# Where the softmax sums stand in a round, and where their division is made: a two-layer graph network on one core

## The chip, the cores and the metric

One core of a Trainium2 chip runs the whole program. The metric is the device time of one execution in microseconds (us). The core has a matrix engine (TensorE, "PE" in the profile), a vector engine (VectorE, "DVE"), a scalar engine (ScalarE, "ACT"), a general engine (GpSimd, "POOL") and a sync engine (SyncE, "SP") that issues DMAs. Each works through its own queue of instructions in order, and they wait for each other by semaphores. TensorE writes its results to PSUM; VectorE and ScalarE read them there[...].

## The reference, cut to what matters

64 independent batches of 256 tokens with 512 features each go through two layers; all arithmetic is float32. H is 8 heads of 64 features.

```
# layer 0: attention with a mask that all batches share
q, k, v = x @ Wq + bq, x @ Wk + bk, x @ Wv + bv          # in 8 heads of 64
scores  = q k^T / 8 + (1 - adj) * -1e9                   # 256 x 256 for each head
attn    = softmax(scores over the keys)
x       = layernorm(x + (attn v) @ Wo + bo)
# layer 1: additive attention, one head
h  = x @ W ;  s1 = h . a[:512] ;  s2 = h . a[512:]
e  = leaky_relu(s1[:, None] + s2[None, :], 0.2) * adj
x  = layernorm(x + elu(softmax(e) h + beta * h))
```

## The kernel before, in words

The program is written as a list of operations per batch. `Plan.op` (L76) records each with its engine, an estimated duration, what it reads and writes, and, for TensorE, a *turn*. `Plan.place` (L107) then puts all operations of all 64 batches into one order, and `emit` writes that order out; on the chip every engine's queue follows it. Three rules of `place` matter:

- TensorE follows the turns strictly (L160) until 70 of its operations are left; those last ones are free. A turn is (round, place in `ROUND`), set by `turn` (L477): `later` says in which round an operation of batch n is done, counted from n, and `ROUND` (L23) in which order within a round.
- Every other operation gets a due time, counted back from the TensorE operations that need it (L123); what no TensorE operation needs is due 15 us after what it reads (L131). Each engine takes what can start first, and among those that can start equally soon the one due first.
- Buffers are taken from slots (L236): 8 PSUM banks (tag "ps"), 9 large tiles in SBUF for xT, qT, kT, V, oT and others, 5 for x, and so on. An operation that finds no slot free waits. A change of TensorE's array shape (the `mode` of an operation) counts 0.25 us.

A round before the change works on four batches at once. In the order of `ROUND`, for round r, with the batch in brackets: mix (r-1), scores (r), o (r-1), spread (r-2), x (r+1), sums (r), v (r), logits (r-1), u (r-2), q (r+1), k (r+1), attention (r-1).

What these are:

- **x**: two blocks of 128 tokens are transposed (`tr_x`, L498), copied out by ScalarE (L501), and GpSimd makes three sums of quarters and a difference in place from them (`token_sums`, L350; L360 in the profile). Later GpSimd adds the bias of the output to x (L503).
- **q, k, v, o, u**: products with the weights, and **spread**: the product of layer 1's attention with x. All six go through `project` (L369): seven products of quarters of the matrices in place of eight (Strassen's scheme in Winograd's form), into three PSUM banks, `ps_chain`, `ps_cross` and `ps_pair`. ScalarE copies and VectorE adds collect the quarters (L519, L522, L528; for o, VectorE adds to x, L702).
- **scores** (two operations, for four heads each): k times q with a contraction of 64, so two matmuls stand side by side in the rows of the array (mode "rows", L576). VectorE adds the mask (L583), ScalarE takes the exponential (L585), and GpSimd adds the two halves of the keys (`both`, L587). Keys lie on the partitions, so a softmax sum is a sum over partitions.
- **sums** (`denominators`, L591): products with a matrix of ones, four side by side (mode "sums", L599), give the softmax sums of the eight heads in one bank, `ps_den`. VectorE takes the reciprocal (L603); ScalarE adds up `ps_den` and the reciprocal for a check of their range (L606); a DMA stores the reciprocals in DRAM (L609), and two more load them back, spread over the partitions, as `inv_all` (`everywhere`, L613).
- **mix** (two operations): attention weights times v, 64 columns a head, two side by side (mode "columns", L553), into `ps_pv`. VectorE multiplies `ps_pv` by `inv_all` on its way out to `oT` (L619); that is the division of the softmax. GpSimd then makes o's sums of quarters from `oT`.
- **logits**: after o, each block of 128 tokens is normalised (`norm`, L455: L458 and L459 on VectorE, L462 and L463 on GpSimd, L466 on VectorE, L468 on ScalarE). VectorE takes four products with sums (L717, into `junk`, with `s` the result). TensorE transposes `s` (`tr_s`, L727), and a chain over L733, L735, L737, L739, L741, L744, L746 makes layer 1's attention.
- **attention**: its transposition (`tr_a`, L755), copied out by ScalarE (L759), with four sums on GpSimd (L770).
- At the end of a batch, after u: L803 to L806, a second `norm`, and the store (L809).

If a check of the sums' range fails, another path (`attention_by_queries`) computes everything again. With these inputs it isn't run.

Of the kernel before, what the change touches and what calls it, by code (L numbers as in the profile page):

```python
# [19 lines left out]
ALPHA = 0.2  # L20
NEG = -1000000000.0

ROUND = ("mix", "scores", "o", "spread", "x", "sums", "v", "logits", "u", "q", "k", "attention")  # L23
SAFE = 1e15


# [196 lines left out]
def gnn_two_layers(ctx: ExitStack, tc: tile.TileContext, x, adj, Wq, bq, Wk, bk, Wv, bv, Wo, bo, W, a, beta, out):  # L223
    nc = tc.nc
# [23 lines left out]
    plan = Plan(slots)  # L248
    stay = []
    A = slice(None)  # L250

    def sb(tag, shape, name):
        return Buf(sb_pool, tag, [P] + shape, name)

    def ps(shape, name):
        return Buf(ps_pool, "ps", [P] + shape, name)
# [11 lines left out]
    def blk(t):  # L268
        return slice(t * P, (t + 1) * P)

    def half(i):
        return slice(i * F, (i + 1) * F)
# [141 lines left out]
    def residual_bias():  # L414
        bo_sb = for_now(bo, 0, "bo")
        acc = ps([D], "ps_b")

        def pe():
            for c in range(C):
                nc.tensor.matmul(acc[A], bv_sb[:, c:c + 1].to_broadcast([P, P]), wo_sb[:, c, :], start=c == 0,  # L420
                                 stop=c == C - 1)

        plan.op("PE", 3440, pe, [wo_sb], [acc], claims=[res_sb])
        plan.op("DVE", 690, lambda: nc.vector.tensor_add(res_sb[A], acc[A], bo_sb[A]), [acc, bo_sb], [res_sb])  # L424
        return weight_sums(wo_sb, "so_sb", "POOL", [res_sb])
# [46 lines left out]
    def batch(b, at, general=False):  # L472

        X = sb("x", [NT, D], f"x_{b}")
        n = b or 0

        def turn(what):  # L477

            later = {"x": -1, "q": -1, "k": -1, "scores": 0, "v": 0, "sums": 0, "mix": 1, "o": 1, "logits": 1,
                     "attention": 1, "spread": 2, "u": 2}[what]  # L480
            plan.turn = (n + later, ROUND.index(what if b != 0 or what != "sums" else "logits"))

        plan.op("SP", 2800, lambda: nc.sync.dma_start(X[A], x[at].rearrange("o (t p) d -> p (o t) d", p=P)), [],
                [(X, (t, i)) for t in range(NT) for i in range(2)], first=b == 0)
# [6 lines left out]
        V = sb("full", [NT, D], f"v_{b}")  # L491
# [14 lines left out]
        if b == 0:  # L506
            plan.turn = (0, ROUND.index("spread"))
            left["o"] = residual_bias()
        turn("x")
        for t in range(NT):  # L510
            tr_x(t)
# [24 lines left out]
        def val():  # L536
            turn("v")
            project(lv, right, False, [V], *gather(lambda q: (lambda: V[:, q[1], half(q[0])], (V, q))))


        oT = sb("full", [C, N], f"oT_{b}")

        def mixed(pT, g, onto, reads=()):

            turn("mix")
            acc = ps([2, N], "ps_pv")

            def pe():
                for i in range(2):
                    for k in range(NT):  # L550
                        for s in range(2):
                            h = 4 * g + 2 * i + s
                            nc.tensor.matmul(acc[s * HD:(s + 1) * HD, i, :], V[:, k, h * HD:(h + 1) * HD],  # L553
                                             pT[h][:, k, :], start=k == 0, stop=k == NT - 1)

            plan.op("PE", 1740, pe, [(V, (g, 0)), (V, (g, 1))] + pT[4 * g:4 * g + 4] + list(reads), [acc],
                    mode="columns", claims=[oT])
            plan.op("DVE", 690, lambda: onto(acc), [acc] + list(reads), [(oT, g)])

        def attention_by_keys():  # L560

            pT = [sb("half", [NT, N], "pT") for h in range(H)]
            both = [sb("half", [2, N], "both") for c in range(C)]
            inv, everywhere = sb("half", [N], "inv"), sb("full", [C, N], "inv_all")
            rows = Buf(dram_pool, "rows", [H, N], "rows")

            def scores(g):
                turn("scores")
                acc = [ps([NT, N], "ps_sc") for _ in range(4)]

                def pe():
                    for i in range(0, 4, 2):
                        for k in range(NT):
                            for s in range(2):
                                h, r = 4 * g + i + s, s * HD
                                nc.tensor.matmul(acc[i + s][:, k, :], kT[r:r + HD, h // 2, blk(k)],  # L576
                                                 qT[r:r + HD, h // 2, :], start=True, stop=True)

                plan.op("PE", 1740, pe, [(m, (g, j)) for m in (qT, kT) for j in range(NT)], acc, mode="rows",
                        claims=pT[4 * g:4 * g + 4] + both[2 * g:2 * g + 2])  # L580
                for i in range(4):
                    h = 4 * g + i
                    plan.op("DVE", 690, lambda h=h, i=i: nc.vector.tensor_add(pT[h][A], acc[i][A], maskT_sb[A]),  # L583
                            [acc[i], maskT_sb], [pT[h]])
                    plan.op("ACT", 620, lambda h=h: nc.scalar.activation(  # L585
                        pT[h][A], pT[h][A], AF.Exp, scale=1.0 / HD ** 0.5), [pT[h]], [pT[h]])
                    plan.op("POOL", 725, lambda h=h: nc.gpsimd.tensor_tensor(  # L587
                        both[h // 2][:, h % 2, :], pT[h][:, 0, :], pT[h][:, 1, :], ALU.add),
                        [pT[h]], [(both[h // 2], h % 2)])

            def denominators():  # L591
                turn("sums")

                acc = ps([N], "ps_den")

                def pe():
                    for s in range(2):
                        for c in range(C):
                            nc.tensor.matmul(acc[32 * c:32 * c + 32, :], ones[:, 16 - 16 * s:48 - 16 * s],  # L599
                                             both[c][:, s, :], start=s == 0, stop=s == 1)  # L600

                plan.op("PE", 1000, pe, both, [acc], mode="sums", claims=[inv])
                plan.op("DVE", 1750, lambda: nc.vector.reciprocal(inv[A], acc[A]), [acc], [inv])  # L603
                for i, m in enumerate((acc, inv)):
                    junk = sb("half", [N], "junk")
                    plan.op("ACT", 600, lambda i=i, m=m, junk=junk: nc.scalar.activation(  # L606
                        junk[A], m[A], AF.Identity, accum_out=range_sb[:, i, b:b + 1]), [m],
                        [junk, (range_sb, (i, b))])
                plan.op("SP", 60, lambda: nc.sync.dma_start(rows[A], inv[0:P:P // H, :]), [inv], [rows])  # L609
                for s in range(2):  # L610
                    def spread(s=s):
                        r = rows[A]
                        nc.sync.dma_start(everywhere[s * HD:(s + 1) * HD], bass.AP(  # L613
                            tensor=r.tensor, offset=r.offset + s * N, ap=[[0, HD], [2 * N, C], [1, N]]))

                    plan.op("SP", 1500, spread, [rows], [(everywhere, s)])

            def mix(g):
                mixed(pT, g, lambda acc: nc.vector.tensor_mul(  # L619
                    oT[:, 2 * g:2 * g + 2, :], acc[A], everywhere[:, 2 * g:2 * g + 2, :]), [everywhere])  # L620

            scores(0)
            scores(1)
            val()
            denominators()
            mix(0)
            mix(1)

        def attention_by_queries():
# [32 lines left out]
            pT = [sb("half", [NT, N], "pT") for h in range(H)]  # L662
# [20 lines left out]
            for g in range(2):  # L683
                for h in range(4 * g, 4 * g + 4):
                    flip(h)
                mixed(pT, g, lambda acc, g=g: nc.vector.tensor_copy(oT[:, 2 * g:2 * g + 2, :], acc[A]))

        turn("q")
        qk(lq, bq_sb, qT)
# [2 lines left out]
        if general:  # L692
            attention_by_queries()
        else:
            attention_by_keys()
# [4 lines left out]
        def onto(q, acc):  # L700
            i, j = q
            plan.op("DVE", 420, lambda: nc.vector.tensor_add(  # L702
                X[:, j, half(i)], X[:, j, half(i)], acc[1]()), [acc[0], (X, (j, i))], [(X, (j, i))])
# [10 lines left out]
        for t in range(NT):  # L714
            for i in range(2):
# [4 lines left out]
                    mode="two")  # L720
# [45 lines left out]
        sums = [(lambda i=i: S[:, i]) for i in range(4)]  # L766
# [27 lines left out]
        u = sb("full", [NT, D], f"u_{b}")  # L794
# [43 lines left out]
    with tc.If(again != 0):  # L838
# [3 lines left out]
        with tc.For_i(0, B, 1) as i:  # L842
            for tile_ in stay:
                tile_.parts = {}
            plan = Plan({**slots, "half": slots["half"] - 1})
# [33 lines left out]
```

## Time and profile before

| | us |
|---|---|
| median of three executions | 2874.97 (2874.73 to 2876.3) |
| the profiled execution: its span | 2874.1 |
| one steady round | 44.07 |

Busy time in the profiled execution:

| engine | busy us | share | instructions |
|---|---|---|---|
| TensorE, matmul | 2838.8 | 99% | 20373 |
| TensorE, weight load | 2489.0 | 87% | 20373 |
| VectorE | 2072.5 | 72% | 4514 |
| ScalarE | 1385.9 | 48% | 3393 |
| GpSimd | 1757.7 | 61% | 2522 |

Lines of the profile name an engine, a line of the kernel, an operation, what it writes and reads, and the shapes as partitions x elements; "x8" means eight instructions. In a timeline the first column is the start and the second the duration; neighbours of one kind are merged into one line. Matmuls overlap in the pipeline, so the time that one group costs is read from its start to the next group's start. DMA moves 39 GB/s on the mean, and the granted TensorE clock is 0.996 of full speed.

### The profile page before, as it was taken

Reading aid. Unit: us, or ns where it says so; the run is one execution under the profiler, and the core shown is the slowest. Engines: PE = TensorE matmul, PEld = TensorE weight load, DVE = VectorE, ACT = ScalarE, POOL = GpSimd, SP = SyncE. Lnnn points to the kernel's source line nnn. Section 1 sums busy time; section 2 is a strip of 40 time slices with the busy share of each in tenths; the row PEclk is TensorE's granted clock in tenths of the full one; section 3 lists DMA queues with packets and bytes.
Section 4 is the critical chain, followed back from the end, with each engine's and each line's share of the span. In section 5 each row is a group of like instructions: output and inputs, shape, how many; then the busy total and the mean of one; then the engine's idle time right before and its main releaser. Section 6 shows DMA issues by size and latency. Waiting matters only on the chain.

```text
span 2874.1 us, 54166 instructions
## 1 busy us (share of the span) xinstructions
PE 2838.8 (99%) x20373; PEld 2489.0 (87%) x20373; DVE 2072.5 (72%) x4514; ACT 1385.9 (48%) x3393; POOL 1757.7 (61%) x2522
## 2 busy tenths in 40 slices
PE   8999999999999999999999999999999999999996
PEld 7888888888888888888888888888888888888885
DVE  5777776776777777767777777677776776776766
ACT  3454544444444445444545454444454445544443
POOL 6665565665655656656656556566565565665654
PEclk9999999999999999999999999999999999999998
DMA  3101111111011110110110111101101111011100
GB/s 133 31 30 38 38 38 38 31 41 42 31 38 41 35 38 33 43 38 30 38 45 31 38 38 38 38 31 38 45 31 38 40 35 38 31 45 38 31 23 30
DMA packets 75417, 111.02 MB, mean 39 GB/s; under 512 B 5904, under 2 KB 39440, under 8 KB 75152
## 3 DMA queue, kind: packets, MB, share of 16 engines
q1 hardware_dynamic: 75024, 107.50, 11.3%
q8 instruction: 163, 2.67, 0.4%
q14 instruction: 102, 0.84, 0.1%
q0 software_dynamic: 128, 0.01, 0.0%
HBM read 73.41 MB, written 34.08 MB: 37 GB/s over the span
## 4 chain that ended last, share of the span: by engine, by line
PE 98%; DVE 1%; POOL 0%; issue 0%; DMA 0%; ACT 0%; POOLq 0%; DVEq 0%
PE ps_chain L387 18%; PE ps_chain L382 15%; PE ps_pair L387 11%; PE ps_cross L387 11%; PE ps_cross L382 10%; PE ps_pair L382 10%; PE ps_sc L576 8%; PE ps_pv L553 8%; PE ps_den L599 2%; PE tr_x L498 2%; PE tr_a L755 1%; PE tr_s L727 1%; DVE junk L717 0%; DMA beta_sb<-in_L_gnn_beta_dram 0%; PE ps_b L420 0%
## 5 line engine op out<-in xcount | busy, mean ns | idle before, releaser
L585 ACT ACTIVATE pT<-pT 128x512 f32<-128x512 f32 x512 | 312.1, 630 | 448.0 <-DVE pT L583 444.3
L587 POOL TENSOR_TENSOR both<-pT 128x256 f32<-128x256 f32 x512 | 357.9, 731 | 24.3 <-ACT pT L585 24.0
L462 POOL TENSOR_SCALAR rs<-mv 128x1 f32<-128x1 f32 x256 | 55.9, 219 | 504.3 <-DVE mv L459 504.3
L583 DVE TENSOR_TENSOR pT<-ps_sc,maskT_sb 128x512 f32<-128x512 f32 x512 | 322.5, 681 | 22.4 <-PE ps_sc L576 22.3
L717 DVE SCALAR_TENSOR_TENSOR junk<-x,wa_sb 128x512 f32<-128x512 f32 x256 | 282.3, 1154 | 0.4 <-ACT x L468 0.3
L770 POOL TENSOR_TENSOR att_sums<-attT 128x128 f32<-128x128 f32 x128 | 58.8, 459 | 323.6 <-ACT attT L759 318.6
L576 PE MATMUL ps_sc<-qT,kT 64*128 64x256 f32 x2048 | 238.4, 382 | 0.0
L468 ACT ACTIVATE x<-x,nmr,rs 128x512 f32<-128x512 f32 x256 | 200.7, 808 | 72.1 <-DVE nmr L466 63.6
L553 PE MATMUL ps_pv<-pT,v 128*64 128x256 f32 x2048 | 235.1, 382 | 0.0
L576 PEld LDWEIGHTS ps_sc<-qT,kT 64*128 64x128 f32 x2048 | 192.8, 187 | 44.1 <-issue 24.2
L553 PEld LDWEIGHTS ps_pv<-pT,v 128*64 128x64 f32 x2048 | 141.3, 137 | 75.4 <-issue 10.4
L619 DVE TENSOR_TENSOR oT<-ps_pv,inv_all 128x512 f32<-128x512 f32 x128 | 88.5, 691 | 163.6 <-PE ps_pv L553 163.6
L458 DVE BATCH_NORM_STATS2 bn<-x 128x6 f32<-128x512 f32 x256 | 164.0, 680 | 2.3
L503 POOL TENSOR_TENSOR x<-x,res_sb 128x512 f32<-128x512 f32 x128 | 160.5, 1276 | 7.3 <-DVE res_sb L424 7.3
L360 POOL TENSOR_TENSOR oS<-oT 128x256 f32<-128x256 f32 x128 | 94.0, 734 | 108.3 <-DVE oT L619 103.3
L463 POOL TENSOR_TENSOR rs<-rs,neg_half 128x1 f32<-128x1 f32 x256 | 144.7, 565 | 21.4
L360 POOL TENSOR_TENSOR xS<-xT 128x256 f32<-128x256 f32 x128 | 140.8, 1100 | 8.1 <-ACT xT L501 3.1
L382 PE MATMUL ps_chain<-xS,sq_sb 128*128 128x128 f32 x1024 | 135.8, 276 | 0.0
L382 PE MATMUL ps_chain<-xS,sk_sb 128*128 128x128 f32 x1024 | 135.2, 275 | 0.0
L702 DVE TENSOR_TENSOR x<-x,ps_chain 128x256 f32<-128x256 f32 x256 | 101.4, 416 | 44.9 <-PE ps_chain L387 38.2
L387 PE MATMUL ps_chain<-so_sb,oS 128*128 128x256 f32 x512 | 131.5, 379 | 0.0
L387 PE MATMUL ps_chain<-sw_sb,yS 128*128 128x256 f32 x512 | 131.5, 379 | 0.0
(192 smaller groups left out, 7546.0 us busy)
## 6 DMA issues: line engine op xcount, KB each, us to landing
x<-in_x_dram SPq DMA_DIRECT2D x64, 512.0 KB, 3.7
inv_all<-rows SPq DMA_DIRECT2D x128, 256.0 KB, 3.6
out_dram<-x SPq DMA_DIRECT2D x128, 256.0 KB, 2.0
wq_sb<-in_L_gnn_Wq_dram SPq DMA_DIRECT2D x1, 1024.0 KB
wk_sb<-in_L_gnn_Wk_dram SPq DMA_DIRECT2D x1, 1024.0 KB
wo_sb<-in_L_gnn_Wo_dram SPq DMA_DIRECT2D x1, 1024.0 KB
wv_sb<-in_L_gnn_Wv_dram SPq DMA_DIRECT2D x1, 1024.0 KB
w_sb<-in_L_gnn_W_dram SPq DMA_DIRECT2D x1, 1024.0 KB, 13.0
```

The costliest lines, as they stand in the source:

```text
L360: plan.op("POOL", 725, lambda: nc.gpsimd.tensor_tensor(dst(), p(), m(), ALU.subtract), reads, writes)
L382: nc.tensor.matmul(dst[:, f, :], l[:, c, blk(f)], r[:, c, :], start=start and f == 0 and c == 0, stop=c == inner - 1, skip_group_check=True)
L387: nc.tensor.matmul(dst, r[:, c, :], l[:, c, :], start=start and c == 0, stop=c == 1, skip_group_check=True)
L458: plan.op("DVE", 690, lambda: nc.vector.bn_stats(bn[A], X[:, t, :]), [(X, (t, 0)), (X, (t, 1))], [bn])
L468: plan.op("ACT", 810, lambda: nc.scalar.activation(X[:, t, :], X[:, t, :], AF.Identity, bias=nm[A], scale=rs[A]), [nm, rs], [(X, (t, 0)), ...
L503: plan.op("POOL", 1270, lambda: nc.gpsimd.tensor_tensor(X[:, t, :], X[:, t, :], res_sb[A], ALU.add), [res_sb], tokens(t))
L553: nc.tensor.matmul(acc[s * HD:(s + 1) * HD, i, :], V[:, k, h * HD:(h + 1) * HD], pT[h][:, k, :], start=k == 0, stop=k == NT - 1)
L576: nc.tensor.matmul(acc[i + s][:, k, :], kT[r:r + HD, h // 2, blk(k)], qT[r:r + HD, h // 2, :], start=True, stop=True)
L583: plan.op("DVE", 690, lambda h=h, i=i: nc.vector.tensor_add(pT[h][A], acc[i][A], maskT_sb[A]), [acc[i], maskT_sb], [pT[h]])
L585: plan.op("ACT", 620, lambda h=h: nc.scalar.activation(pT[h][A], pT[h][A], AF.Exp, scale=1.0 / HD ** 0.5), [pT[h]], [pT[h]])
L587: plan.op("POOL", 725, lambda h=h: nc.gpsimd.tensor_tensor(both[h // 2][:, h % 2, :], pT[h][:, 0, :], pT[h][:, 1, :], ALU.add), [pT[h]], [ ...
L717: plan.op("DVE", 780, lambda t=t, i=i, junk=junk: nc.vector.scalar_tensor_tensor(junk[A], X[:, t, :], 1.0, wa_sb[:, i, :], op0=ALU.mult, o ...
```

## The change

Four edits. `ROUND` and `later` are new: the order in round r becomes sums (r-1), mix (r-1), scores (r), q (r+1), attention (r-2), v (r), spread (r-2), o (r-1), u (r-2), k (r+1), x (r+2), logits (r-1). So the sums stand directly in front of the mix of the same batch, attention is transposed in the same round as spread's products, and x is transposed a round earlier. A special case for the first batch's sums goes. The mix no longer reads `everywhere`: ScalarE copies `ps_pv` to `oT`, and VectorE multiplies `oT` by `everywhere` in place, in SBUF (mode "two": the plan lets it not overlap with GpSimd). In the path that isn't run the copy is recorded from another place in the code.

```diff
--- before.py
+++ after.py
@@ -20,7 +20,7 @@
 ALPHA = 0.2
 NEG = -1000000000.0
 
-ROUND = ("mix", "scores", "o", "spread", "x", "sums", "v", "logits", "u", "q", "k", "attention")
+ROUND = ("sums", "mix", "scores", "q", "attention", "v", "spread", "o", "u", "k", "x", "logits")
 SAFE = 1e15
 
 
@@ -476,9 +476,9 @@
 
         def turn(what):
 
-            later = {"x": -1, "q": -1, "k": -1, "scores": 0, "v": 0, "sums": 0, "mix": 1, "o": 1, "logits": 1,
-                     "attention": 1, "spread": 2, "u": 2}[what]
-            plan.turn = (n + later, ROUND.index(what if b != 0 or what != "sums" else "logits"))
+            later = {"x": -2, "q": -1, "k": -1, "scores": 0, "v": 0, "sums": 1, "mix": 1, "o": 1, "logits": 1,
+                     "attention": 2, "spread": 2, "u": 2}[what]
+            plan.turn = (n + later, ROUND.index(what))
 
         plan.op("SP", 2800, lambda: nc.sync.dma_start(X[A], x[at].rearrange("o (t p) d -> p (o t) d", p=P)), [],
                 [(X, (t, i)) for t in range(NT) for i in range(2)], first=b == 0)
@@ -540,7 +540,7 @@
 
         oT = sb("full", [C, N], f"oT_{b}")
 
-        def mixed(pT, g, onto, reads=()):
+        def mixed(pT, g, onto):
 
             turn("mix")
             acc = ps([2, N], "ps_pv")
@@ -553,9 +553,9 @@
                             nc.tensor.matmul(acc[s * HD:(s + 1) * HD, i, :], V[:, k, h * HD:(h + 1) * HD],
                                              pT[h][:, k, :], start=k == 0, stop=k == NT - 1)
 
-            plan.op("PE", 1740, pe, [(V, (g, 0)), (V, (g, 1))] + pT[4 * g:4 * g + 4] + list(reads), [acc],
+            plan.op("PE", 1740, pe, [(V, (g, 0)), (V, (g, 1))] + pT[4 * g:4 * g + 4], [acc],
                     mode="columns", claims=[oT])
-            plan.op("DVE", 690, lambda: onto(acc), [acc] + list(reads), [(oT, g)])
+            onto(acc)
 
         def attention_by_keys():
 
@@ -616,8 +616,14 @@
                     plan.op("SP", 1500, spread, [rows], [(everywhere, s)])
 
             def mix(g):
-                mixed(pT, g, lambda acc: nc.vector.tensor_mul(
-                    oT[:, 2 * g:2 * g + 2, :], acc[A], everywhere[:, 2 * g:2 * g + 2, :]), [everywhere])
+                part = slice(2 * g, 2 * g + 2)
+
+                def onto(acc):
+                    plan.op("ACT", 590, lambda: nc.scalar.copy(oT[:, part, :], acc[A]), [acc], [(oT, g)])
+                    plan.op("DVE", 690, lambda: nc.vector.tensor_mul(
+                        oT[:, part, :], oT[:, part, :], everywhere[:, part, :]), [everywhere], [(oT, g)], mode="two")
+
+                mixed(pT, g, onto)
 
             scores(0)
             scores(1)
@@ -683,7 +689,8 @@
             for g in range(2):
                 for h in range(4 * g, 4 * g + 4):
                     flip(h)
-                mixed(pT, g, lambda acc, g=g: nc.vector.tensor_copy(oT[:, 2 * g:2 * g + 2, :], acc[A]))
+                mixed(pT, g, lambda acc, g=g: plan.op("DVE", 690, lambda: nc.vector.tensor_copy(
+                    oT[:, 2 * g:2 * g + 2, :], acc[A]), [acc], [(oT, g)]))
 
         turn("q")
         qk(lq, bq_sb, qT)
```

## The prediction

> **What bounds the kernel now.** I read the page's chain of waits first: which engine holds the end.
>
> ```profile
> PE 98%; DVE 1%; POOL 0%; issue 0%; DMA 0%; ACT 0%; POOLq 0%; DVEq 0%
> ```
>
> TensorE alone. So only two things move the time: what TensorE itself spends between matmuls, and any new wait in its queue. I then read one steady round in TensorE's timeline (start us, us, line, operands); starts matter, since the printed durations overlap.
>
> ```profile
> 1402.25 1.05 PE L382 MATMUL ps_chain<-xT,wq_sb 128*128 128x128 f32 x8
> ...
> 1414.75 0.60 PE L755 MATMUL tr_a<-ident,e 128*128 128x128 f32 x4
> 1415.28 3.67 PE L553 MATMUL ps_pv<-pT,v 128*64 128x256 f32 x32
> 1418.89 3.72 PE L576 MATMUL ps_sc<-qT,kT 64*128 64x256 f32 x32
> 1422.54 1.13 PE L387 MATMUL ps_chain<-wo_sb,oT 128*128 128x256 f32 x4
> 1423.51 1.03 PE L387 MATMUL ps_cross<-wo_sb,oT 128*128 128x256 f32 x4
> 1424.37 1.03 PE L387 MATMUL ps_pair<-wo_sb,oT 128*128 128x256 f32 x4
> ...
> 1431.81 1.04 PE L498 MATMUL tr_x<-ident,x 128*128 128x128 f32 x8
> 1432.78 1.07 PE L599 MATMUL ps_den<-both,ones 128*32 128x256 f32 x16
> 1433.78 1.13 PE L387 MATMUL ps_chain<-wv_sb,xT 128*128 128x256 f32 x4
> 1434.75 1.03 PE L387 MATMUL ps_cross<-wv_sb,xT 128*128 128x256 f32 x4
> ...
> 1439.93 0.51 PE L727 MATMUL tr_s<-ident,s 128*128 128x128 f32 x2
> 1440.27 1.03 PE L387 MATMUL ps_chain<-w_sb,yT 128*128 128x256 f32 x4
> ...
> 1446.32 1.05 PE L382 MATMUL ps_chain<-xT,wq_sb 128*128 128x128 f32 x8
> ```
>
> A round is 1446.32 - 1402.25 = 44.07 us, and 61 rounds repeat it. Four ordinary matmuls of 256 columns take 0.86 (1423.51 to 1424.37), but the four just after the scores 0.97, and the four after the sums 0.97: a change of array shape costs time. From the single records: an ordinary start-to-start gap is 0.216 (256 columns) or 0.110 (128). Above that, summed over the two gaps at each change: full to columns (into the mix) 0.143, columns to rows 0.206, rows to full 0.201, full to sums 0.117, sums to full 0.217. Five changes, 0.88 a round. One more loss is at tr_s: 0.34 for two transposes of 0.11, 0.12 too much. The waits view names it (us in total, times, longest):
>
> ```profile
> PEld tr_s L727 <- DVE junk L717: 22.9, 65, 2.5
> ```
>
> Every round the second transpose waits for the last VectorE product of L717. Last, the table by stretches (first the mix and scores, then from sums to v):
>
> ```profile
> 1414.75:1422.54 7.79, 7.79 (x70) 5.58 (x69) 4.63 (x9) 2.35 (x4) 4.36 (x8) 1.00 0.30 103
> 1432.78:1439.93 7.15, 7.15 (x46) 5.79 (x45) 6.97 (x11) 4.09 (x11) 6.68 (x9) 1.00 0.14 41
> ```
>
> VectorE (the third busy column) is full, 6.97 of 7.15, just where L717 comes late, though it is 72% busy overall. That is the engine to watch.
>
> [...] L717 takes 0.69 alone (at 2808.80) and 1.20 beside GpSimd, whose xS rows are 1.10 there against 0.73 for the same shape in yS. [...] 8 banks. The two scores operations take four each, so they need all of them; the trace shows no wait for that now. [...] in the trace L606 starts on ps_den only 0.03 after the reciprocal L603 ends.
>
> **The change, part by part.**
>
> Sums next to the mix. The order becomes (full) sums, mix, scores (full): four changes instead of five. Sums to full (0.217) and full to columns (0.143) go; sums to columns comes, which no row shows. Below: full to columns, 0.143; above: sums to full, 0.217; near to columns to rows, 0.206. I take 0.19. Saved 0.360 - 0.19 = 0.17 a round (0.14 to 0.22); over 63 rounds 10.7 us (9 to 14).
>
> Longer road to tr_s. Now o ends at 1428.69 and tr_s comes at 1439.93: 11.2 us between (spread 3.1, x 1.0, sums 1.0, v 6.1). After it, u (6.0), k (6.2) and x (0.9) lie between: 13.1. The chain misses by 0.07 today, and in the new stretch neither the reciprocal (1.76) nor the v adds sit before L717. The wait goes: 0.12 x 62 = 7.4 us (0 if the order puts other VectorE work ahead).
>
> Other distances shrink; need against room, from the same rows. x to q: room 13.5 before, now tr_s 0.3, sums 1.0, mix 3.6, scores 3.65, so 8.6; need 1.1 (two copies L501) + 4 x 1.1 (xS) + lags 0.5 = 6.0, and only half of it for the first two products. tr_s to tr_a: 18.6, now 14.5; L746 ends 8.7 after tr_s. tr_a to spread: 13.4, now v 6.0; need 0.6 (L759) + 4 x 0.53 = 2.9. spread to u: 8.5, now o 6.0; yS ends 4.3 after spread. sums to o: need 2.0 to the reciprocal's end, 3.0 to the last spread DMA's issue, 3.6 to its landing, 1.4 to 2.4 for the division, 3.2 for oS, 14 in all; room mix, scores, q, tr_a, v, spread, 23. All hold: nothing on the path.
>
> Division in SBUF. 128 ScalarE copies at L759's 0.586 come new: 75 us, or 48% to 51% of ScalarE, beside TensorE. They free ps_pv about as soon as L619 did (0.69). The 128 multiplications stay; with two SBUF inputs they cost at best 0.68, at worst L717's 1.20, so VectorE and GpSimd each get 0 to 1.0 us more to do a round, at about 11 to 13 us after the sums, where o is still 10 us off: nothing. The mix no longer waits for the spread DMAs, which it didn't show as waiting for. SP's queue holds the same five issues a round and waits behind the same producers; x's load has a fifth slot: X lives four rounds and 8 us of the five that its slots allow. In the other path (L686) the copy is only moved, and that path isn't run: nothing.
>
> Ends. At the start tr_s waits 1.5 (80.15); with 13 us of room it won't: -1.5, kept at 0 to -3. At the end order is free for the last 70 TensorE operations. There the mix waits for the DMAs and the last o stands 3.08 after it (2819.44). The new mix runs sooner, but sums may be placed later since shape changes are put off: -2, between -6 and +5.
>
> Sum: 2874.1 - 10.7 - 7.4 - 1.5 - 2 = 2852.5. The unprofiled median stands 0.9 above that span (2874.97), so 2853.4; I add half a microsecond or so for small new waits: **2854**.
>
> **The rivals.**
>
> A. A bank instead of a drain: the slower side. The sums' bank ps_den must be free when the second scores operation starts, 6.45 after the sums (1.0 + 3.6 + half of 3.65), because that one needs the last four banks. With VectorE free it is: now reciprocal ends 2.9 after the sums' start, and L606 lets go at 3.4. So the reciprocal may stand 3.0 us in VectorE's queue. What is ahead of it: the last k adds 0.7, the previous u's bn_stats 1.3, z 0.9, e 0.7, small ones 0.4. That is 4.0, of which about 1.6 runs before the sums end: late by 2.4, with 0.6 in hand. Behind the reciprocal stand the pT additions that free the scores' banks for q. Between o's end and tr_a, I count VectorE: norm 2.1, L717 4.7, u and k adds 3.0, u's end 4.6, z to L746 4.4, reciprocal 1.8, pT 5.0, q adds 1.5: 27 in some 28 us. For it: this crowding, and that sums were before v, where banks were plenty. Against: the plan weighs banks and drains, and the late half of u's end can slip. Each microsecond over 3.0 costs 62 us; it eats the 0.29 gain from 0.29 over. At 0.5 over: 2854 + 31 = 2885; at 1.0 over: 2916.
>
> B. Only the drain is saved: L717 is late again, with u's and k's adds or u's end ahead of it. 2854 + 7.4 = 2861.
>
> C. The drain is a fixed price of each group, so sums to columns costs the whole 0.36, and the waits move about. With B's loss as well nothing is left: 2872. Against it: columns to rows, also between two divided shapes, costs 0.206 and not 0.36.
>
> D. The order written isn't the order run: the planner could stretch the steady rounds. But TensorE follows the turns strictly until the last 70, so that the order itself is kept is near certain.
>
> **How the numbers follow.** Forecast 0.52, its own range 2846 to 2860. B 0.18. A 0.22, spread 2862 to 2920: 0.03 of it still faster, 0.02 no change. C 0.08: 0.01 faster, 0.04 no change. 0.2% is 5.7 us, about what a measurement of this kernel can tell from no change. Faster: 0.52 + 0.17 (B) + 0.03 + 0.01 = 0.73; same: 0.01 + 0.02 + 0.04 = 0.07; slower: 0.17 + 0.03 = 0.20. For 8 in 10, leave out some 5% below and 13% above: 2845 to 2892.
>
> **What would show it.** Right: a round of about 43.78; the gap from sums to the mix about 0.19 above 0.216 over two gaps; tr_s in 0.22; no wait of TensorE on L603, L606 or L583. A: TensorE waits before the second half of L576 or at q's first products. B: L717 again ends tr_s's wait. The forecast is wrong if a round is over 43.95, or if the last mix-to-end stretch grows by over 5.

## The result, and the profile after

| | before | after |
|---|---|---|
| median of four executions each, us | 2875.09 (2874.73 to 2876.3) | 2855.7 (2855.0 to 2856.15) |
| span of the profiled execution, us | 2874.1 | 2853.2 |
| one steady round, us | 44.064 | 43.767 |
| VectorE busy, us | 2072.5 | 2101.7 |
| ScalarE busy, us | 1385.9 | 1406.8 |
| GpSimd busy, us | 1757.7 | 1801.5 |

The changed kernel is faster: ratio 0.9932, with an interval of 0.9914 to 0.9949. Lines of `after.py` below the new `onto` have moved by a few numbers: the copy of `ps_pv` is L622, the multiplication L623, L717 is now L724, `tr_s` L734, L746 is L753 and `tr_a` L762.

The chain of waits of the changed kernel, by engine:

```profile
PE 98%; DVE 1%; DMA 0%; ACT 0%; issue 0%; POOL 0%; DVEq 0%; POOLq 0%; SPq 0%; ACTq 0%
```

It is still TensorE alone, so the gain must lie between its matmuls. One steady round in TensorE's timeline of the changed kernel, with the places where the change acts:

```profile
1402.22 1.04 PE L498 MATMUL tr_x<-ident,x 128*128 128x128 f32 x8
1403.09 0.38 PE L734 MATMUL tr_s<-ident,s 128*128 128x128 f32 x2
1403.40 1.07 PE L599 MATMUL ps_den<-both,ones 128*32 128x256 f32 x16
1404.40 3.67 PE L553 MATMUL ps_pv<-pT,v 128*64 128x256 f32 x32
1408.01 3.72 PE L576 MATMUL ps_sc<-qT,kT 64*128 64x256 f32 x32
1411.66 1.16 PE L382 MATMUL ps_chain<-xT,wq_sb 128*128 128x128 f32 x8
1412.65 1.06 PE L382 MATMUL ps_cross<-xT,wq_sb 128*128 128x128 f32 x8
...
1418.45 1.03 PE L387 MATMUL ps_chain<-wv_sb,xT 128*128 128x256 f32 x4
1419.32 1.03 PE L387 MATMUL ps_cross<-wv_sb,xT 128*128 128x256 f32 x4
...
1446.86 0.38 PE L734 MATMUL tr_s<-ident,s 128*128 128x128 f32 x2
```

Three shapes now follow each other (128\*32, 128\*64, 64\*128) with nothing of the full shape between. Only q's first product after the scores still pays for a change on its far side, 0.99 us to the next start against 0.89 ordinarily; v's first product takes 0.87, the ordinary 0.86 to 0.87, where it took 0.97 before. `tr_s` takes 0.31 to the start of the sums: 0.11 for each transpose and 0.09 for the first half of the change to the sums. There is no wait in it.

From the single records, what a round of each kernel loses above its ordinary gaps (0.216 us for 256 columns, 0.110 for 128). The prediction calls what a change of shape costs a drain; what the records show are these longer gaps:

| place | before | after |
|---|---|---|
| full to sums | 0.117 | 0.117 |
| sums to full | 0.217 | |
| full to columns | 0.143 | |
| sums to columns | | 0.164 |
| columns to rows | 0.206 | 0.206 |
| rows to full | 0.201 | 0.201 |
| wait at `tr_s` | 0.120 | 0 |
| wait at spread's sixth product | 0 | 0.02 |
| sum | 1.004 | 0.708 |

The difference of the sums, 0.296, is that of the rounds, 44.064 - 43.767 = 0.297. The rest of the span: the third batch's scores start 2.1 us sooner (96.95 before, 94.84 after), from there to the last batch's scores the kernel gains 18.5, and after that 0.3. Together 20.9, the difference of the spans. Of the 18.5, 61 rounds of 0.297 are 18.1. The last of these rounds is another 0.87 shorter, because no x is left to transpose (x runs a round ahead now, so the start holds one more), and three single rounds are 0.17 to 0.21 us longer than the others.

The stretches of the changed kernel, sums to the middle of the scores and k to `tr_s` (columns: us; busy of TensorE, weight loads, VectorE, ScalarE, GpSimd; clock, DMA share, GB/s):

```profile
1403.40:1409.83 6.43, 6.43 (x65) 4.28 (x66) 6.23 (x13) 3.30 (x10) 6.11 (x10) 1.00 0.01 4
1439.73:1446.86 7.13, 7.13 (x66) 7.13 (x65) 6.83 (x16) 3.79 (x11) 3.64 (x5) 1.00 0.00 1
```

VectorE is as full as it was (6.23 of 6.43; 6.83 of 7.13). What has changed is what stands behind it. VectorE's timeline of the changed kernel shows the two results that TensorE could have waited for:

```profile
1406.28 1.73 DVE L603 RECIPROCAL inv<-ps_den 128x256 f32<-128x256 f32 x1
...
1415.10 0.88 DVE L753 SCALAR_TENSOR_TENSOR e<-e,rc,diag_sb 128x256 f32<-128x256 f32 x2
...
1418.56 1.76 DVE L623 TENSOR_TENSOR oT<-oT,inv_all 128x512 f32<-128x512 f32 x2
...
1442.67 0.08 DVE L724 DVE_READ_ACCUMULATOR junk<-x,wa_sb 128x1 f32 x1
```

The last product of L724 is complete at 1442.75 and `tr_s` comes at 1446.86: 4.1 us in hand, where it was late by 0.07 before. L753 is done 2.0 us before `tr_a` (1415.98, 1418.02). The reciprocal ends 4.6 us after the sums began, and the multiplications end at 1420.3, seven before o begins at 1427.64.

### The profile page after: what moved, and what is told of

Read it like the earlier page. It is cut to its first block, busy times and chain, and to the rows that moved or that the text cites. A ratio compares the mean times of both kernels' runs of the same rounds, so it can differ in the third digit from the quotient of the medians.

```text
span 2853.2 us, 54675 instructions
## 1 busy us (share of the span) xinstructions
PE 2819.2 (99%) x20373; PEld 2493.1 (87%) x20373; DVE 2101.7 (74%) x4514; ACT 1406.8 (49%) x3521; POOL 1801.5 (63%) x2522
## 4 chain that ended last, share of the span: by engine, by line
PE 98%; DVE 1%; DMA 0%; ACT 0%; issue 0%; POOL 0%; DVEq 0%; POOLq 0%; SPq 0%; ACTq 0%
PE ps_chain L387 17%; PE ps_chain L382 15%; PE ps_pair L387 12%; PE ps_cross L387 11%; PE ps_cross L382 10%; PE ps_pair L382 10%; PE ps_sc L576 8%; PE ps_pv L553 8%; PE ps_den L599 2%; PE tr_x L498 2%; PE tr_a L762 1%; PE tr_s L734 0%; DMA beta_sb<-in_L_gnn_beta_dram 0%; DVE junk L724 0%; DMA inv_all<-rows 0%
## 5 line engine op out<-in xcount | busy, mean ns | idle before, releaser
L587 POOL TENSOR_TENSOR both<-pT 128x256 f32<-128x256 f32 x512 | 361.1, 732 | 150.7 <-ACT pT L585 150.7
L583 DVE TENSOR_TENSOR pT<-ps_sc,maskT_sb 128x512 f32<-128x512 f32 x512 | 316.7, 680 | 8.9 <-PE ps_sc L576 3.1
L519 ACT COPY u<-ps_chain 128x256 f32<-128x256 f32 x128 | 47.7, 372 | 519.3 <-PE ps_chain L387 519.3
L585 ACT ACTIVATE pT<-pT 128x512 f32<-128x512 f32 x512 | 287.1, 624 | 4.7 <-DVE pT L583 4.7
L724 DVE SCALAR_TENSOR_TENSOR junk<-x,wa_sb 128x512 f32<-128x512 f32 x256 | 261.8, 1075 | 0.0
L468 ACT ACTIVATE x<-x,nmr,rs 128x512 f32<-128x512 f32 x256 | 193.8, 805 | 7.7 <-DVE nmr L466 7.7
L360 POOL TENSOR_TENSOR yS<-yT 128x256 f32<-128x256 f32 x128 | 93.1, 727 | 157.6 <-DVE yT L528 151.2
L777 POOL TENSOR_TENSOR X_sums<-x 128x256 f32<-128x256 f32 x128 | 122.1, 954 | 84.7 <-ACT x L468 84.7
L458 DVE BATCH_NORM_STATS2 bn<-x 128x6 f32<-128x512 f32 x256 | 170.2, 687 | 4.2
L622 ACT COPY oT<-ps_pv 128x512 f32<-128x512 f32 x128 | 75.0, 586 | 152.3 <-PE ps_pv L553 152.2
```

The lines of the kernel that those rows point to most:

```text
L458: plan.op("DVE", 690, lambda: nc.vector.bn_stats(bn[A], X[:, t, :]), [(X, (t, 0)), (X, (t, 1))], [bn])
L468: plan.op("ACT", 810, lambda: nc.scalar.activation(X[:, t, :], X[:, t, :], AF.Identity, bias=nm[A], scale=rs[A]), [nm, rs], [(X, (t, 0)), ...
L585: plan.op("ACT", 620, lambda h=h: nc.scalar.activation(pT[h][A], pT[h][A], AF.Exp, scale=1.0 / HD ** 0.5), [pT[h]], [pT[h]])
L587: plan.op("POOL", 725, lambda h=h: nc.gpsimd.tensor_tensor(both[h // 2][:, h % 2, :], pT[h][:, 0, :], pT[h][:, 1, :], ALU.add), [pT[h]], [ ...
L724: plan.op("DVE", 780, lambda t=t, i=i, junk=junk: nc.vector.scalar_tensor_tensor(junk[A], X[:, t, :], 1.0, wa_sb[:, i, :], op0=ALU.mult, o ...
```

## The experiments

Each is one edit, on the kernel before or on the changed one. Ratios are against the kernel before.

### The division in SBUF alone

`ROUND` and `later` as before, the division as in the changed kernel (the diff is against the changed kernel):

```diff
-ROUND = ("sums", "mix", "scores", "q", "attention", "v", "spread", "o", "u", "k", "x", "logits")
+ROUND = ("mix", "scores", "o", "spread", "x", "sums", "v", "logits", "u", "q", "k", "attention")
-            later = {"x": -2, ..., "sums": 1, ..., "attention": 2, ...}[what]
+            later = {"x": -1, ..., "sums": 0, ..., "attention": 1, ...}[what]
```

> The division in SBUF alone, with the order of the work as in the kernel before. My theory: the copies on ScalarE and the multiplications with two SBUF inputs lie beside TensorE, and the wait of the mix for the spread DMAs wasn't one, so the time stays: 2875, within 3 (0.999 to 1.001 of before). Rival[...]: each multiplication blocks GpSimd by up to 0.5 us twice a round and the last product of L717 comes later still: up to 2906. Rival, the division is the gain: 2856.

Measured: 2875.94 us, ratio 1.0006 (0.9998 to 1.0014), a round of 44.06. The 128 copies on ScalarE and the slower multiplication (760 ns each on the mean here, 691 before) cost nothing in a round, and they bring nothing by themselves. That a multiplication holds GpSimd up by 0.5 us was the author's estimate (before, L717 takes 0.69 us alone and 1.20 beside GpSimd); the time of this run shows nothing of it.

### The order alone

The kernel before with the new `ROUND`, `later` and turn, and the division still on the way out of PSUM:

```diff
-ROUND = ("mix", "scores", "o", "spread", "x", "sums", "v", "logits", "u", "q", "k", "attention")
+ROUND = ("sums", "mix", "scores", "q", "attention", "v", "spread", "o", "u", "k", "x", "logits")
...
```

> The new order alone, with the division still on the way out of PSUM, so that the mix waits for the spread DMAs. My theory: the mix stands 1.0 us behind the sums' start, and the reciprocals are back as inv_all 9.5 us after it at best (reciprocal's end at 2.9, then 6.6 to the second spread DMA's landing, from the trace of before): 8.5 us of TensorE wait a round, 63 rounds, +535, so 3390, up to 3500 if the reciprocal stands in VectorE's queue as in the changed kernel. Rival: part of it is hidden behind q, which stands behind the mix: under 3100.

Measured: 3327.91 us, ratio 1.1577 (1.1554 to 1.16), a round of 51.20. The time is some 60 us under the expected range and far over the rival's 3100, and the wait is not where it was expected. TensorE's timeline of this run:

```profile
1637.10 1.07 PE L599 MATMUL ps_den<-both,ones 128*32 128x256 f32 x16
1638.10 3.67 PE L553 MATMUL ps_pv<-pT,v 128*64 128x256 f32 x32
1641.71 2.86 PE L576 MATMUL ps_sc<-qT,kT 64*128 64x256 f32 x24
1649.49 2.67 PE L576 MATMUL ps_sc<-qT,kT 64*128 64x256 f32 x8 [4.92 <-DVE oT L619]
```

The mix does not wait at all, although the plan lists `everywhere` among its reads: the matmuls read only V and pT. The scores do, after 24 of their 32 matmuls, for 4.92 us, and after that TensorE is slower: the last 8 matmuls take 2.67 us where the first 24 take 2.86, and the mean granted clock of the run is 0.932 against 0.996 before. VectorE's timeline of the same run:

```profile
1638.77 1.76 DVE L603 RECIPROCAL inv<-ps_den 128x256 f32<-128x256 f32 x1 [0.71 <-ACT junk L606]
...
1647.96 0.88 DVE L746 SCALAR_TENSOR_TENSOR e<-e,rc,diag_sb 128x256 f32<-128x256 f32 x2
1648.76 1.28 DVE L619 TENSOR_TENSOR oT<-ps_pv,inv_all 128x512 f32<-128x512 f32 x2
1649.96 3.66 DVE L583 TENSOR_TENSOR pT<-ps_sc,maskT_sb 128x512 f32<-128x512 f32 x6
```

L619 needs `inv_all`, which has first to be computed, stored and loaded again, and until L619 has run the mix's two results hold their banks, which the scores need. L619 also stands behind L746 in VectorE's queue. The DMA packets in the trace tell the two apart: the last of the 512 packets of 1024 bytes that fill `inv_all` ends at 1646.72, and L619 starts 2.04 us later. In the program's last round, where no L746 stands in front of it, it starts 0.8 us after the last packet. So the queue accounts for some 1.2 us of the wait and the way of the reciprocals for the rest. What the division in SBUF buys is then plain: ScalarE's copy L622 reads only `ps_pv`, so the banks come free without `inv_all`. Alone it is worth nothing, and without it the new order costs 453 us. Not all of that is idle time: of the 7.4 us that a round of this run is longer than a round of the changed kernel, 5.1 are the wait, and most of the rest is the slower pace after it (2.60 us from the start of the last 8 matmuls to q's, at 1652.09, where 8 matmuls of the scores take 0.91 in the changed kernel).

### The sums in front, the rest of the order as before

The kernel of the first experiment, with the sums moved in front of the mix, so that o follows the scores directly:

```diff
-ROUND = ("mix", "scores", "o", "spread", "x", "sums", "v", "logits", "u", "q", "k", "attention")
+ROUND = ("sums", "mix", "scores", "o", "spread", "x", "v", "logits", "u", "q", "k", "attention")
-            later = {..., "sums": 0, ...}[what]
+            later = {..., "sums": 1, ...}[what]
```

> The kernel before with the division in SBUF and the sums in front of the mix, but nothing else of the new order: o still follows the scores. My theory: the division needs some 14 us from the sums' start until oS is made (from the trace of before), and o comes after 8.3 us, so TensorE waits some 4 to 7 us at o a round (o's first product needs only the first half of oT): +250 to +440, 3130 to 3310; the rest of the new order is what makes room. Rival: the drain alone could be had without it: 2864.

Measured: 3389.09 us, ratio 1.179 (1.1766 to 1.1813), a round of 52.17: a wait where it was expected, but the time is above the expected range. TensorE's timeline of this run:

```profile
1619.13 3.72 PE L576 MATMUL ps_sc<-qT,kT 64*128 64x256 f32 x32
1625.92 1.97 PE L387 MATMUL ps_chain<-wo_sb,oT 128*128 128x256 f32 x4 [3.06 <-DVE oT L623]
1629.70 2.08 PE L387 MATMUL ps_cross<-wo_sb,oT 128*128 128x256 f32 x4 [1.82 <-POOL oT L360]
1631.57 1.66 PE L387 MATMUL ps_pair<-wo_sb,oT 128*128 128x256 f32 x4
1633.06 1.03 PE L387 MATMUL ps_chain<-so_sb,oS 128*128 128x256 f32 x4
1633.92 1.03 PE L387 MATMUL ps_cross<-so_sb,oT 128*128 128x256 f32 x4
```

o waits 3.06 us for the multiplication and 1.82 for GpSimd's sums, 4.9 together and so within the 4 to 7 expected. The range left out that what follows is slower: the first three groups show 1.97, 2.08 and 1.66 us where the next show 1.03, and the mean granted clock of the run is 0.925 against 0.996 before. From 1633.06 on a group takes 0.86 to 0.87 to the next start again, the ordinary time. So q, `tr_a`, v and spread between the scores and o are a necessary part of the change: they cover the way of the sums to `oT`.

### The wait at `tr_s` alone

The kernel before, with the four products of L717 over 256 of the 512 features:

```diff
-                    junk[A], X[:, t, :], 1.0, wa_sb[:, i, :], op0=ALU.mult, op1=ALU.mult,
+                    junk[:, 0:F], X[:, t, 0:F], 1.0, wa_sb[:, i, 0:F], op0=ALU.mult, op1=ALU.mult,
```

> The kernel before with L717's four products over 256 of the 512 features, the order unchanged: it leaves out half of layer 1's logits, so that VectorE is through earlier. It isolates the wait of tr_s. Theory: that wait[...], 0.12 us a round, goes: 2875 - 7.4 = 2867.5. Rival, the wait moves to another place as when tr_s stood behind u: 2875 or more.

Measured: 2864.29 us, ratio 0.9966 (0.9954 to 0.9979), a round of 43.943, so 0.121 less than before. TensorE's timeline of this run at `tr_s`:

```profile
1434.31 1.03 PE L387 MATMUL ps_chain<-sv_sb,xS 128*128 128x256 f32 x4
1435.18 0.38 PE L727 MATMUL tr_s<-ident,s 128*128 128x128 f32 x2
1435.39 1.03 PE L387 MATMUL ps_chain<-w_sb,yT 128*128 128x256 f32 x4
```

`tr_s` takes 0.21 to the next start, where it took 0.34. The wait of 0.07 was worth 0.12: the two gaps that it lengthened, 0.180 and 0.159 before, are 0.109 each here. By the medians the run gains 9.95 us, more than the 7.4 expected; in the two traces the difference is 12.0, of which 7.4 lie in the rounds, 1.1 before the third batch's scores and 3.5 after the last batch's. So in a round the wait was worth what was expected; what the ends gained is not broken down.

### `tr_s` put behind u, in the old order

```diff
-ROUND = ("mix", "scores", "o", "spread", "x", "sums", "v", "logits", "u", "q", "k", "attention")
+ROUND = ("mix", "scores", "o", "spread", "x", "sums", "v", "u", "logits", "q", "k", "attention")
```

> The kernel before with tr_s behind u in place of in front of it, nothing else: five changes of shape, division in PSUM. My theory: L717 then has 17.2 us in place of 11.2, its wait (0.12 us a round) goes, and tr_a still has 12.5 of the 8.7 it needs: 2875 - 0.12 x 62 = 2867.6. Rival: the wait only moves to the next operation that is late (tr_a, or u's banks): 2875, within 1.

Measured: 2879.36 us, ratio 1.0018 (1.0011 to 1.0026), a round of 44.160: slower by 0.095, not faster by 0.12. The rival had the mechanism, a wait that moves, but not the place or the size. TensorE's timeline of this run:

```profile
1436.88 1.13 PE L387 MATMUL ps_chain<-wv_sb,xT 128*128 128x256 f32 x4
...
1439.62 1.13 PE L387 MATMUL ps_chain<-sv_sb,xS 128*128 128x256 f32 x4
1440.59 1.03 PE L387 MATMUL ps_cross<-sv_sb,xT 128*128 128x256 f32 x4
...
1449.22 0.38 PE L727 MATMUL tr_s<-ident,s 128*128 128x128 f32 x2
```

The wait at `tr_s` is gone, but v's fourth product now takes 0.97 in place of 0.87. It writes `ps_chain` again, and ScalarE must first have copied v's first product out of it. The waits of weight loads in this run name that copy (us in total, times, longest):

```profile
PEld ps_chain L387 <- ACT v L519: 17.6, 61, 0.3
```

ScalarE's timeline shows why that copy is late:

```profile
1438.83 0.38 ACT L606 ACTIVATE junk<-ps_den 128x256 f32<-128x256 f32 x1 [1.44 <-DVE inv L603]
...
1439.20 0.36 ACT L519 COPY v<-ps_chain 128x256 f32<-128x256 f32 x1
```

The plan had put L606 in front of it, and L606 waited 1.44 us for `ps_den` until the reciprocal had gone through VectorE's queue. Another 0.06 goes at spread's sixth product. So a longer road to `tr_s` is not enough; the order has to leave the banks' copies free as well.

### The sums taken from the mix again, in the new order

In the changed kernel, the sums a round sooner and behind x:

```diff
-ROUND = ("sums", "mix", "scores", "q", "attention", "v", "spread", "o", "u", "k", "x", "logits")
+ROUND = ("mix", "scores", "q", "attention", "v", "spread", "o", "u", "k", "x", "sums", "logits")
-            later = {..., "sums": 1, ...}[what]
+            later = {..., "sums": 0, ...}[what]
```

> The changed kernel with the sums one place earlier, in front of tr_s, so that tr_s (full array) stands between the sums and the mix: five changes of shape in place of four, all else within 0.3 us of its place. My theory, a price for each change: full to sums 0.117, sums to full 0.217, full to columns 0.143 in place of full to sums 0.117 and sums to columns 0.164, so +0.196 us a round, 63 rounds, +12.3: 2868. Rival C, a price for each group of divided matmuls whatever stands next to it: no change, 2856.

Measured: 2926.24 us, ratio 1.0178 (1.0164 to 1.0192), a round of 44.84, 1.07 more than after, and several times what was expected. Around the sums the gaps grew by 0.146 only. The other 0.925 is at `tr_a`. TensorE's timeline of this run there, and VectorE's in front of it:

```profile
1407.01 0.55 PE L762 MATMUL tr_a<-ident,e 128*128 128x128 f32 x3 [0.48 <-DVE e L753]
```

```profile
1400.90 1.67 DVE L623 TENSOR_TENSOR oT<-oT,inv_all 128x512 f32<-128x512 f32 x2
1402.49 2.47 DVE L583 TENSOR_TENSOR pT<-ps_sc,maskT_sb 128x512 f32<-128x512 f32 x4
...
1405.55 1.41 DVE L753 SCALAR_TENSOR_TENSOR e<-e,rc,diag_sb 128x256 f32<-128x256 f32 x2
```

With the sums earlier the multiplications L623 could start earlier, and the plan put them in front of the mask additions and of L753, for which `tr_a` then waits in every round. (After, L753 comes 3.5 us before L623.) The edit changed two things, so it doesn't measure a drain. The next one does.

### The same, with every other engine's queue unchanged

The plan of the changed kernel is made as it is, and then each sums operation changes places with the `tr_s` in front of it, on TensorE only. Sums then stand between transposes:

```diff
     order = plan.place()
+    for n in [n for n in order if plan.ops[n][5] == "sums"]:
+        at = order.index(n)
+        before = next(i for i in range(at - 1, -1, -1) if plan.ops[order[i]][0] == "PE")
+        if plan.ops[order[before]][2].__name__ == "pe_row":
+            assert all(order.index(d) < before for d in plan.ops[n][3])
+            order.insert(before, order.pop(at))
```

> The changed kernel with the sums put in front of tr_s after the plan is made, so that on TensorE alone two neighbours change places and every other engine keeps its order (the run that let the plan do it also reordered VectorE, and tr_a then waited 0.9 us a round). It isolates the drain. Theory: the gaps around the sums grow from 0.989 to 1.135 us, as the records of that run show, so +0.146 a round, 62 rounds: +9.1, 2865. Rival, a price for each group and not for each change: 2856.

Measured: 2864.19 us, ratio 0.9965 (0.9952 to 0.9979), a round of 43.911, 0.1445 more than after. TensorE's timeline of this run:

```profile
1406.04 1.04 PE L498 MATMUL tr_x<-ident,x 128*128 128x128 f32 x8
1407.01 1.07 PE L599 MATMUL ps_den<-both,ones 128*32 128x256 f32 x16
1408.01 0.43 PE L734 MATMUL tr_s<-ident,s 128*128 128x128 f32 x2
1408.37 3.67 PE L553 MATMUL ps_pv<-pT,v 128*64 128x256 f32 x32
```

From `tr_x` to the scores there are 5.94 us here (1411.98 the next start) and 5.79 after, with the same 58 matmuls. So the price is paid at each change of shape and not for each group. It is 0.146 and not 0.196 because of what follows the sums. The gap over the change is 0.113 too long in each case; the gap behind it is 0.104 too long where v's products of 256 columns come next, as before the change, and 0.05 where transposes or the mix do. What decides between 0.104 and 0.05 is not shown. It is not the number of columns: q's first product, of 128 columns like the transposes, has 0.103 behind the scores, and the mix, of 256, has 0.05. The round of this experiment shows 0.1445; the 0.196 of the change itself is read from the records of the two traces.

### x first in the round

In the changed kernel, "x" at the head of `ROUND` and `"x": -1` in place of -2. TensorE's queue has the same cycle, but the cycle starts at another place.

> The changed kernel with x transposed at the start of the next round (later -1, first in the order) in place of the end of this one: by the round's count not sooner than before, by the place in TensorE's queue only behind tr_s in place of in front of it. My theory: transposing a round sooner is a matter of counting, and this is the changed kernel: 2856, within 2. Rival: the earlier transposition gives part of the gain: over 2860.

Measured: 2857.96 us, ratio 0.9943 (0.993 to 0.9957), a round of 43.767, the same to the last digit. The 2 us lie at the start, once. The first `tr_s` that waits in the changed kernel, and then in this one:

```profile
89.98 0.32 PE L734 MATMUL tr_s<-ident,s 128*128 128x128 f32 x1 [0.33 <-DVE junk L724]
```

```profile
91.41 0.32 PE L734 MATMUL tr_s<-ident,s 128*128 128x128 f32 x1 [1.94 <-DVE junk L724]
```

"A round sooner" is then a matter of where a round is counted from; what matters is the cycle.

### The reciprocal, two and three times as long

In the changed kernel the reciprocal is made twice, or three times, within its one operation of the plan, so that no queue changes its order:

```diff
-                plan.op("DVE", 1750, lambda: nc.vector.reciprocal(inv[A], acc[A]), [acc], [inv])
+                plan.op("DVE", 1750, lambda: [nc.vector.reciprocal(inv[A], acc[A]) for _ in range(2)], [acc], [inv])
```

> The changed kernel with the reciprocal L603 done twice, the plan's order unchanged. It tests rival A. In the trace of the changed kernel ps_den comes free 4.6 us after the sums' start and is wanted at 6.43; tr_a's chain has 2.0 us in hand. One more reciprocal (1.65 us) leaves 0.2: theory 2856 to 2868. Rival, VectorE is already the limit behind the reciprocal: +1.65 a round, 2956 or more.

> The changed kernel with the reciprocal done three times. Theory: ps_den comes free at 7.9 in place of the wanted 6.43, so TensorE waits 1.5 to 1.9 us a round before the second scores operation: +95 to +120, 2950 to 2976. Rival, VectorE is 26% idle and takes 3.3 us a round without loss: 2856 to 2862.

Measured: twice 2863.26 us, ratio 0.996 (0.9946 to 0.9975), a round of 43.855, within the expected range; three times 2979.56, ratio 1.0365 (1.0344 to 1.0386), a round of 45.649, 3.6 us above it. TensorE's timeline with three:

```profile
1415.81 1.07 PE L599 MATMUL ps_den<-both,ones 128*32 128x256 f32 x16
...
1420.41 3.29 PE L576 MATMUL ps_sc<-qT,kT 64*128 64x256 f32 x26
1424.06 1.13 PE L576 MATMUL ps_sc<-qT,kT 64*128 64x256 f32 x6 [0.36 <-DVE nmr L466]
1425.35 1.16 PE L382 MATMUL ps_chain<-xT,wq_sb 128*128 128x128 f32 x8 [0.16 <-DVE pT L583]
...
1428.66 1.02 PE L382 MATMUL ps_chain<-xS,sq_sb 128*128 128x128 f32 x7 [0.37 <-POOL both L587]
```

and VectorE's:

```profile
1418.70 5.31 DVE L603 RECIPROCAL inv<-ps_den 128x256 f32<-128x256 f32 x3
```

The scores stop after 26 matmuls and go on at 1424.06, when the third reciprocal has ended (1424.01). The trace names L466, the next instruction on VectorE, but the bank is the reciprocal's. The scores come to this bank late, since only their last matmuls write to it: in the changed kernel the weight load that waits for it starts at 1410.49, 7.1 us after the sums began. With the unchanged reciprocal the bank is free after 4.6, so 2.5 us are in hand. With two reciprocals it is free after 6.4, and the scores don't wait. With three it is free after 8.2, 1.1 too late, and from the start of the scores to the start of q it takes 1.28 us longer than in the changed kernel. The 0.088 that two cost lie at q's fourth product, which takes up `ps_chain` again after ScalarE's copy L522: that copy ends at 1417.41 and the product starts at 1417.55, and it stands in ScalarE's queue behind work that VectorE delivers later. With three the same place costs 0.6 (L522 ends at 1428.52, the product starts at 1428.66; L587, which the trace names, had ended at about the same time). Apart from spread's sixth product, which already waits 0.02, this is the nearest limit that these runs found in the changed kernel, with some 0.75 us in hand: there L522 ends at 1413.55 and the product starts at 1414.44, of which 0.14 is the ordinary way from one to the other.

## Why the prediction was right

The forecast was 2854, the time 2855.7, and its mechanism is the one that the runs show. Step by step:

**The drain.** 0.17 a round was expected, 0.196 measured. The one number that no row showed, sums to columns, was taken as 0.19 and is 0.164. Over 63 rounds this is 12.3 us in place of 10.7. The exchange of sums and `tr_s` shows that it is the change of shape that costs, and that a part of the price depends on what follows. The forecast's 0.217 for sums to full therefore holds in front of v; in front of `tr_s` it is 0.163.

**The wait at `tr_s`.** 0.120 expected, 0.120 measured in the two traces, and 0.121 in the experiment that takes that wait away alone. The two parts make the whole: 0.121 + 0.196 - 0.02 = 0.297. The reason given, the longer road, was right here, but isn't sufficient by itself: with only `tr_s` moved, the wait went to v's fourth product. That none came in the changed order was a matter of how the whole order lies. The forecast listed the distances to operands, and not the way from each product of a group to the copy that frees its bank.

**Distances that shrink.** None of them became a wait. The division was put at 1.4 to 2.4 us for its two products and takes 1.76 (929 ns each on the mean against 691 before), and it ends seven us ahead of o.

**The division at nothing.** Right: 1.0006 alone. What the forecast said of its effect, that the mix no longer waits for the spread, was beside the point: the mix never waits for it on the chip. What the division does is free the banks, and without it the new order costs 7.4 us a round more. The copies took the 75 us that the forecast gave them, but ScalarE's busy time rose by only 20.9, to 49% and not 51%: the durations together rose by 72 (1545.6 to 1617.7), but busy time counts overlapping instructions once.

**Ends.** Start -1.5 expected, -2.1 measured up to the third batch's scores; 1.2 of that is the wait at `tr_s` (1.52 before, 0.33 after), and the rest is not broken down here. End -2 expected, -0.3 measured. The small new waits, half a microsecond allowed, came to 1.2 (0.02 a round at spread's sixth product), and the three longer rounds to 0.55.

**The sum.** The trace gives 18.5 for the rounds, 2.1 for the start and 0.3 for the end: 20.9, so a span of 2853.2, against 2852.5 forecast. By the forecast's own terms the rounds come to 12.3 + 7.4 - 1.2 = 18.5 as well, but its counts of 62 and 63 rounds reach into the two ends, so that this agrees to a tenth is chance. So is a part of the closeness of the total: the drain saved 1.6 more than forecast, and the end 1.7 less. The rest of the 1.7 us between 2854 and 2855.7 is how the median stands to the profiled span: 2.5 above it after, 0.9 before.

**Rival A, the bank of the sums.** Its mechanism is real: with the reciprocal three times as long TensorE stops at just that bank, and from two to three each added microsecond costs about one a round (1.75 us added, 1.79 measured: 1.28 up to q's start, 0.5 more at q's fourth product). Three terms were mis-sized. The reciprocal stood 1.7 us in VectorE's queue (its start is 2.88 after the sums', and the sums are complete after some 1.1), not 2.4. L606, which the forecast put behind the reciprocal and gave 0.5 us, now reads `ps_den` in front of it (1404.60, the reciprocal 1406.28). And the scores want the bank at 7.1 us and not at 6.45, because the second operation fills its four banks one after the other. The chance of 0.22 was given to a margin of 0.6 us that was in truth 2.5.

**Rival B, only the drain.** It didn't come; L724 has 4.1 us in hand. **Rival C, a price for each group.** It is refuted by the exchange of sums and `tr_s`. **Rival D, the order.** TensorE's order is as written, but the run with the sums a round sooner shows that the *other* queues can shift with a step of one place, and by more (0.925 us a round) than the drain that was to be measured.

## What to carry to other kernels

When one engine holds the end, list its gaps one by one and give each a cause: here five changes of shape and one wait made the whole account of a round, and the gain was read from it before the change was built. Before putting a producer next to its consumer, ask what the consumer's result does until its late operand comes: a result that waits in PSUM holds banks (in the order alone the scores waited 4.92 us a round for them), so copy it out first and finish it in SBUF. To measure one cause in a planned program, change the finished order and not the plan's input, since a planner moves the other queues as well (here for 0.925 us a round at `tr_a`).

## What had not been expected of the hardware

- A wait of TensorE cost twice where it was read from the records. The gap that waits is longer, and so is the next: 0.180 and 0.159 at `tr_s` before against 0.109, and 0.267 and 0.320 at v's fourth product in the run with `tr_s` behind u, against 0.216. The second part was 0.05 at the transposes and 0.104 at products of 256 columns; at q's fourth product, of 128 columns, it was 0.074 with the reciprocal made twice.
- A change of shape shows two such parts. The second was 0.024 in front of the sums, 0.05 in front of transposes and the mix, 0.104 in front of the scores and of products of 256 columns, and 0.103 in front of q's, of 128; what decides it stays open. One change fewer was worth 0.146 us a round in the exchange of sums and `tr_s`, and 0.196 in the change itself.
- After an idle time TensorE could run at half pace. With the sums in front and o behind the scores, 3.06 us of idle time were followed by groups of 1.97, 2.08 and 1.66 us in place of 1.03 (from 1625.92 to 1633.06), with a second idle time of 1.82 in between; the mean granted clock of that run was 0.925 against 0.996. The length alone doesn't decide. Near the end of the changed kernel 2.57 us of idle time were followed by a granted clock of 0.50 and single gaps of 0.43 for 0.216 (from 2798.5 on, for 2.5 us), and 1.42 us by a clock of 0.50 as well (from 2818.8 on, for 2.5 us); near the start of the kernel before, 1.52 us were followed by 1.00 (from 80.15 on, for 2.5 us). What decides it is not shown.
